# Attention scores of pass 2: from TensorE products to a VectorE turn, a DRAM reload and ScalarE's bias

## The chip, the core and the metric

One core of a Trainium2 chip. Its engines run side by side, each through its own list of instructions in order: TensorE (PE: matmuls, with weight loads, PEld, that overlap them), VectorE (DVE), ScalarE (ACT), GpSimd (POOL) and SyncE (SP), which here issues DMAs. They wait for each other by semaphores. The metric is the device time of one execution in microseconds (us), less is better. Before the change it is 2358.47 us, the median of three runs (2357.71 to 2360.64).

## What is computed

Two layers on `x` of 128 graphs x 64 nodes x 768 features, f32. Layer 0 is a graph convolution with relations; the change doesn't touch it. Layer 1 is graph attention with six heads of 128 features and a gate:

```python
h = jnp.einsum('bni,hio->bhno', feat_in, W)
th = jnp.tanh(h)
attn_src = jnp.einsum('bhno,hoz->bhnz', th, w_src)
attn_dst = jnp.einsum('bhno,hoz->bhnz', th, w_dst)
attn = attn_src + jnp.swapaxes(attn_dst, -1, -2)
attn = jnp.where(attn >= 0, attn, leaky_alpha * attn)
mask = (adj == 0)[:, None, :, :]
attn = jnp.where(mask, NEG_MASK, attn)
attn = jax.nn.softmax(attn, axis=-1)
feat_out = jnp.einsum('bhnm,bhmo->bhno', attn, h) + b
...
feat_out = jax.nn.elu(feat_out)
gate = jax.nn.sigmoid(feat_in @ H_w.T + H_b)
out = gate * feat_out + (1.0 - gate) * feat_in
```

A score is thus a sum: the source node's number plus the destination node's number, per head and graph, then leaky ReLU, mask and softmax over the 64 destinations.

## The kernel before

The 8192 nodes are 64 tiles of 128 rows (two graphs each), and two tiles are a pair: 32 pairs. Pass 1 (layer 0, up to about 1410 us) runs over all pairs and writes its results to DRAM. Pass 2 (layer 1) runs over the pairs again. Its work is cut into named steps, and one text, `ORDER` (line 104), gives the order in which they are issued in every iteration `i`: `name/k` means that the step is done for pair `i - k`. So an iteration works on several pairs at different stages. The list is complete (every step falls on a real pair) from iteration 4 to 29; `END` (line 122) is a second list for the last pairs. Steps of one engine run in the order of the list; between engines only data, buffers and semaphores decide. `FINISH` places the end of pass 1's last pair within the first iterations.

The steps, for a pair or, where a digit 0 or 1 follows the name, for one of its tiles:

- `ld` (load, load_h, lines 373 and 987): eight DMAs of 96 KB that bring a pair's transposed input h from DRAM in 128-byte pieces, and one for the adjacency `ai`. The step with pair p loads pair p + 1.
- `Ff..` (form, 1048): sums of input blocks on DVE. `P k.q` (half_product, 1055): 30 half products of 128x512 a pair on PE, 15 products by a fast-multiplication scheme for h and the gate together. They accumulate in PSUM banks a (two buffers), b, c and d, one bank running through several products: products 0, 3, 6, 9 and 12 use bank a. `R k` and `RA k` (read on DVE, 1077; read_act on ACT, 1073) read a bank between two of its products.
- `th` tanh on ACT (1095); `mul` one DVE product with both score vectors (1099); `sum` (1106): ACT's accumulating copies, `sum..0` and `sum..1` for the destination scores, `sum..2` and `sum..3` for the source scores.
- The scores: `k`, `chain` (1113, 1117, POOL): the scores split in three bf16 parts that add up to f32; `rows` (1139, PE): one bf16 matmul that turns them into rows; `rrow` (DVE) and `lrow` (ACT) lay the rows out as operands; `log` (1159, PE): one bf16 matmul that gives all scores of the tile, 128x384, in PSUM; `memset` (POOL) fills the mask's value, `cp` (1165, DVE) copies the unmasked scores over it; `pre` (1170, ACT) is the leaky ReLU.
- `tr` the negative maximum (DVE), `exp` (1178, ACT, six activations of 128x64 with sums), `rec` (DVE); `tv`, `ts`, `tl` (1201 to 1216): the weights are turned in 32x32 blocks on DVE, put to DRAM by four DMAs and loaded back turned, for the next step.
- `swap` (1126): two DMAs that swap the two graphs' halves of h; `att` (1242): 24 small matmuls with the pair's weights; `ev` (1254): twelve DVE evictions of 128x128, divided by the softmax sums; `e`, `g` on ACT; `f` (1273): three DVE steps; `lx` (996) loads the residual; `dma` (1284, POOL) adds the result to the output in DRAM.

Every DMA issue of SP takes its place in one queue: an issue whose data isn't ready holds all that stand behind it. Steps that the prediction follows by name: `P9.0`, `R6`, `R9`, `R12`, `att`, `ev`, `ld`, `Ff1`, `lx`, `ts`, `swap`, `tl`, `f1.2`, `f0.2`.

Of the kernel before, what the change touches and what calls it, by code (L numbers as in the profile page):

```python
# [101 lines left out]


ORDER = """
dma0/4 R1/1 RA1/1 P3.1/1 R2/1 memset1/2 R14/2 th1/2 R3/1 tv1/3 P11.0/1 rows0/2 P4.0/1 rrow0/2
lrow0/2 tl0/3 mul1/2 P6.0/1 Ff1 P4.1/1 R4/1 Ff6/1 log0/2 P6.1/1 P11.1/1 sum1.2/2 R6/1 sum1.3/2
sum1.0/2 Ff7 sum1.1/2 P7.0/1 k1/2 cp0/2 Ff4 lx1/3 P7.1/1 rec0/3 Ff2 P9.0/1 Ff8 Ff11/1 R7/1 P9.1/1
pre0/2 RA7/1 tr0/2 chain1/2 P8.0/1 Ff9 P8.1/1 R9/1 lx0/3 rows1/2 Ff10 memset0/1 ld R11/1 g1/3
exp0.0/2 ts1/3 rrow1/2 R8/1 P10.0/1 P10.1/1 exp0.1/2 Ff3 swap0/3 lrow1/2 th0/1 P12.0/1 tv0/2 R10/1
P12.1/1 mul0/1 tl1/3 g0/2 att/3 log1/2 R12/1 ev1.0/3 ev1.1/3 cp1/2 sum0.3/1 ev0.0/3 sum0.1/1 P13.0/1  # L110
e1/3 f1.0/3 P13.1/1 P14.0/1 sum0.0/1 P14.1/1 P2.0 P2.1 R13/1 ev0.1/3 P1.0 pre1/2 f1.1/3 sum0.2/1
tr1/2 f1.2/3 P0.0 P0.1 e0/3 dma1/3 P5.0 f0.0/3 swap1/2 P5.1 exp1.0/2 RA0 R0 P1.1 exp1.1/2 f0.1/3
ts0/2 RA5 k0/1 chain0/1 rec1/2 Ff5 RA14/1 P3.0 f0.2/3 R5 RA2
""".split()
# [3 lines left out]
END = """
g0/3 R1/2 R2/2 R14/3 Ff6/2 P3.1/2 Ff1/1 P11.0/2 R3/2 RA1/2 P4.0/2 rows0/3 P4.1/2 tv1/4 P6.0/2 th1/3
Ff11/2 rrow0/3 R4/2 lrow0/3 mul1/3 Ff4/1 sum1.2/3 P6.1/2 lx0/4 dma0/5 P7.0/2 rec0/4 sum1.1/3
sum1.0/3 P7.1/2 P8.0/2 log0/3 R6/2 Ff2/1 Ff8/1 Ff3/1 Ff7/1 Ff9/1 ts1/4 R7/2 swap0/4 P8.1/2 P9.0/2
k1/3 sum1.3/3 tl1/4 RA7/2 P9.1/2 Ff5/1 chain1/3 P11.1/2 R8/2 g1/3 P10.0/2 rows1/3 cp0/3 Ff10/1
pre0/3 P10.1/2 lrow1/3 R9/2 tr0/3 R11/2 memset1/3 th0/2 tl0/4 rrow1/3 att/4 log1/3 P12.0/2 P12.1/2
R10/2 P13.0/2 lx1/4 P13.1/2 mul0/2 exp0.0/3 ev1.0/4 ev1.1/4 sum0.3/2 ev0.0/4 ev0.1/4 e1/4 e0/4
sum0.2/2 P5.0/1 memset0/2 R12/2 g0/2 f1.0/4 cp1/3 P2.0/1 g1/4 P0.0/1 exp0.1/3 Ff6/1 swap1/3 f1.1/4
P14.0/2 P0.1/1 R13/2 pre1/3 f0.0/4 P14.1/2 sum0.0/2 f1.2/4 P1.0/1 f0.1/4 P2.1/1 R0/1 sum0.1/2 f0.2/4  # L130
RA0/1 RA2/1 R14/2 P1.1/1 RA1/1 P5.1/1 ld/1 P3.0/1 Ff11/1 R2/1 tr1/3 RA14/2 R1/1 RA5/1 R5/1 th1/2
tv0/3 mul1/2 exp1.0/3 P3.1/1 P8.0/1 Ff1 P8.1/1 exp1.1/3 k0/2 P4.0/1 dma0/4 chain0/2 tv1/3 ts0/3
sum1.1/2 rows0/2 rrow0/2 R3/1 sum1.2/2 lx1/3 P4.1/1 Ff2 Ff4 P11.0/1 lrow0/2 Ff5 P6.0/1 sum1.0/2
sum1.3/2 log0/2 P6.1/1 R4/1 k1/2 P7.0/1 cp0/2 Ff8 pre0/2 R6/1 P7.1/1 tr0/2 P9.0/1 exp0.0/2 ts1/3
R8/1 dma1/4 Ff3 P9.1/1 memset1/2 Ff9 rec0/3 R7/1 Ff10 Ff7 exp0.1/2 tv0/2 chain1/2 tl0/3 rows1/2
RA7/1 lrow1/2 P11.1/1 rrow1/2 lx0/3 P10.0/1 log1/2 swap0/3 tl1/3 R9/1 rec1/3 P10.1/1 R11/1 cp1/2
R10/1 th0/1 att/3 pre1/2 P13.0/1 mul0/1 sum0.3/1 ev1.1/3 ev0.0/3 memset0/1 sum0.1/1 sum0.2/1
sum0.0/1 lx0/2 ev1.0/3 ts0/2 ev0.1/3 P13.1/1 k0/1 P12.0/1 P12.1/1 tr1/2 chain0/1 R13/1 swap1/2 PH2
swap0/2 e1/3 R12/1 e0/3 PH0 P14.0/1 P14.1/1 f1.0/3 f0.0/3 f1.1/3 exp1.0/2 R14/1 exp1.1/2 tv1/2 PH5
f1.2/3 rows0/1 f0.1/3 RA14/1 lrow0/1 RAH0 dma1/3 f0.2/3 PH1 PG0 PH3 ts1/2 th1/1 RAH5 RAH1 RAH2  # L140
mul1/1 PH11 dma0/3 tl0/2 PH4 RH3 lx1/2 memset1/1 Ff6 sum1.0/1 RH4 Ff11 tl1/2 sum1.1/1 PH6 rrow0/1
PH7 RH6 sum1.3/1 RAH7 log0/1 PH9 RG0 sum1.2/1 cp0/1 RH9 pre0/1 rec0/2 RH11 PH8 RH8 PH10 th0 k1/1
chain1/1 rows1/1 att/2 lrow1/1 tr0/1 exp0.0/1 exp0.1/1 rec1/2 RH10 mul0 rrow1/1 PH13 log1/1 ev0.0/2
ev0.1/2 tv0/1 PH12 sum0.3 ev1.1/2 cp1/1 lx0/1 sum0.2 e0/2 sum0.0 pre1/1 RH12 ts0/1 f0.0/2 PG2 PH14
sum0.1 k0 RG2 PG3 RH13 tr1/1 PG1 PG8 swap0/1 exp1.0/1 ev1.0/2 f0.1/2 exp1.1/1 chain0 tl0/1 RAH14 RG3
rec0/1 rows0 PG6 f0.2/2 RG1 memset0 th1 swap1/1 tv1/1 e1/2 mul1 f1.0/2 rec1/1 lx0 f1.1/2 lrow0 PG4
g1/2 att0/1 rrow0 sum1.1 PG5 log0 dma0/2 f1.2/2 ev0.0/1 sum1.0 sum1.2 memset1 RG6 cp0 sum1.3 pre0
ts1/1 lx1/1 tl1/1 RG4 k1 chain1 rows1 ev0.1/1 e0/1 RG5 tr0 PG7 rrow1 lrow1 f0.0/1 g0/1 RG7 log1
f0.1/1 swap0 att1/1 PG11 cp1 exp0.0 f0.2/1 dma1/2 ev1.0/1 PG9 exp0.1 ev1.1/1 RG9 g1/1 swap1 pre1
turnp0 dma0/1 e1/1 tr1 PG10 PG12 RG10 f1.0/1 rec0 pT0 att0 f1.1/1 f1.2/1 exp1.0 RG12 PG14 RG8 exp1.1  # L150
ev0.1 turnp1 e0.1 rec1 PG13 ev0.0 f0.0.1 e0.0 RG14 RG11 RG13 pT1 f0.1.1 f0.0.0 g0 dma1/1 att1 f0.2.1
f0.1.0 lx1 ev1.1 g1 ev1.0 e1.1 f1.0.1 e1.0 f1.1.1 f1.0.0 f1.2.1 f1.1.0 f1.3.1 f1.2.0 f1.3.0 f0.2.0
out1.1 out0.1 out1.0 out0.0
""".split()


# [1 line left out]
def kernel(  # L158
# [90 lines left out]

# [153 lines left out]
    with ExitStack() as px:  # L403
        wa = px.enter_context(tc.tile_pool(name="wa", bufs=1))
        work = px.enter_context(tc.tile_pool(name="work0", bufs=2))
# [573 lines left out]
    with ExitStack() as px:  # L979
        wb = px.enter_context(tc.tile_pool(name="wb", bufs=1))  # L980
        work = px.enter_context(tc.tile_pool(name="work1", bufs=2))
# [225 lines left out]
        def put_blocks(t):  # L1207

            for f in range(NQ):
                nc.sync.dma_start(  # L1210
# [73 lines left out]
        def store(t):  # L1284
# [176 lines left out]
```

## Time and profile before

The profiled execution took 2358.5 us, its span from first to last instruction 2356.7 us. The granted TensorE clock was 0.994 over the span.

| view | PE | DVE | ACT | POOL |
|---|---|---|---|---|
| busy over the whole span, us | 2326.5 | 1979.0 | 1304.5 | 434.1 |
| share of the span | 99% | 84% | 55% | 18% |

| group in pass 2 | engine | mean of one, ns |
|---|---|---|
| half product's record, 128x512 f32 (two for each half product) | PE | 592 |
| `log`, 128x384 bf16, 64 of them | PE | 331 |
| `rows`, 128x192 bf16, 64 of them | PE | 249 |
| `mul`, 128x1536 | DVE | 1732 |
| `ev`, 128x128 | DVE | 331 |
| `rrow`, 64x384 | DVE | 531 |
| `cp`, 128x384 | DVE | 575 |
| `tv`, transpose of 128x384 | DVE | 567 |
| `exp`, 128x64 | ACT | 337 |
| `pre`, 128x384 | ACT | 509 |
| `lrow`, 18x128 | ACT | 257 |
| store to the output, issue | POOL | 887 |

A record's length is the time until its result is there; instructions of one engine overlap, so the distance from start to start is shorter (DVE by about 0.08 us). A timeline line gives the start, the length of a run of equal instructions, the engine, line, operation and tiles; `x4` means four of them. SPq and POOL with DMA_DIRECT2D are the issues of DMAs, not their transfers. The DMA queue that SP fills moved 269.11 MB in 696850 packets, its packets took 46.5% of the 16 DMA engines' span; POOL's queue took 6.0% with 24.78 MB.

### The profile page before, as it was taken

The page shows a single profiled execution, that of the slowest core. Times are in us where ns is not written, and L with a number is a line of the kernel's source. Part 1 is how long each engine was busy: PE and PEld are TensorE (multiplying, and loading weights), DVE is VectorE, ACT ScalarE, POOL GpSimd, SP SyncE. Part 2 cuts the span into 40 slices and gives each one's busy share as a digit, 9 for nine tenths or more (in the row PEclk, how much of TensorE's full clock was granted, in tenths as well). Part 3 has the DMA queues.
Part 4 walks back from the last instruction along what each step waited for, and adds up shares of the span by engine and source line. Part 5 has one row for each costly group of instructions (what it writes and reads, how often), then busy time and mean ns, then how long its engine had stood idle before and what let it go on. Part 6 is the DMA issues. An engine that isn't in the chain of part 4 may idle for free.

```text
span 2356.7 us, 35546 instructions
## 1 busy us (share of the span) xinstructions
PE 2326.5 (99%) x11591; PEld 1654.2 (70%) x11591; DVE 1979.0 (84%) x3673; ACT 1304.5 (55%) x3955; POOL 434.1 (18%) x983
## 2 busy tenths in 40 slices
PE   9999999999999999999999999999999999999996
PEld 7888888888888888888888885444444444444444
DVE  8878778777787787787787777899999999999997
ACT  3454454454554554554554533677766776777775
POOL 1111111111111111111111111122222222222222
PEclk9999999999999999999999999999999999999997
DMA  6334435335335335335334357577777776676776
GB/s 188 83 90 125 119 90 136 106 90 143 100 93 147 93 97 152 90 96 147 90 103 139 90 162 145 117 146 142 152 144 150 141 148 140 138 145 138 148 136 132
DMA packets 706907, 296.19 MB, mean 126 GB/s; under 512 B 524586, under 2 KB 657053, under 8 KB 706722
## 3 DMA queue, kind: packets, MB, share of 16 engines
q1 hardware_dynamic: 696850, 269.11, 46.5%
q0 software_dynamic: 9728, 24.78, 6.0%
q8 instruction: 91, 1.49, 0.3%
q14 instruction: 94, 0.77, 0.1%
q10 hardware_dynamic: 144, 0.04, 0.0%
HBM read 131.85 MB, written 136.45 MB: 114 GB/s over the span
## 4 chain that ended last, share of the span: by engine, by line
PE 94%; DVE 2%; DMA 2%; issue 1%; ACT 0%; SPq 0%; POOL 0%; POOLq 0%; DVEq 0%; ACTq 0%
PE pwa L754 21%; PE pwb L754 17%; PE pwcd L754 14%; PE pma L1059 13%; PE pmb L1059 11%; PE pmd L1059 5%; PE pmc L1059 4%; PE pb L682 3%; PE ps L1224 1%; PE pwcd L738 1%; PE pwcd L682 1%; DVE weights L353 1%; PE ps L1163 1%; DMA weights<-in_wrev_t_dram 1%; PE pmc L1224 0%
## 5 line engine op out<-in xcount | busy, mean ns | idle before, releaser
L754 PE MATMUL pwa<-weights,op 128*128 128x256 f32 x2304 | 539.4, 381 | 0.3 <-DVE x L746 0.3
L754 PEld LDWEIGHTS pwa<-weights,op 128*128 128x128 f32 x2304 | 422.3, 190 | 53.8 <-issue 1.1
L754 PE MATMUL pwb<-weights,op 128*128 128x256 f32 x1932 | 454.5, 381 | 0.0
L754 PEld LDWEIGHTS pwb<-weights,op 128*128 128x128 f32 x1932 | 359.4, 190 | 53.1 <-issue 0.2
L353 DVE TENSOR_TENSOR op<-op 128x768 f32<-128x768 f32 x310 | 291.5, 949 | 95.6 <-ACT op L692 91.7
L754 PE MATMUL pwcd<-weights,op 128*128 128x256 f32 x1560 | 357.8, 379 | 0.0
L754 PEld LDWEIGHTS pwcd<-weights,op 128*128 128x128 f32 x1560 | 296.1, 190 | 40.1
L1059 PE MATMUL pma<-weights,op_f 128*128 128x512 f32 x620 | 291.2, 592 | 0.0
L1111 ACT ACTIVATE pr<-pr 128x128 f32<-128x128 f32 x768 | 225.6, 295 | 92.3 <-DVE pr L1101 90.5
L692 ACT COPY op<-pb 128x512 f32<-128x512 f32 (+1 forms) x132 | 70.8, 618 | 320.5 <-PE pb L682 320.5
L1059 PEld LDWEIGHTS pma<-weights,op_f 128*128 128x128 f32 x620 | 117.7, 190 | 147.4 <-issue 139.0
L330 POOL TENSOR_SCALAR rn<-su 128x1 f32<-128x1 f32 x124 | 28.1, 227 | 901.9 <-ACT hf L325 531.0
L1059 PE MATMUL pmb<-weights,op_f 128*128 128x512 f32 x372 | 180.9, 594 | 0.0
L540 ACT ACTIVATE hp<-x,rn 128x768 f32<-128x768 f32 x60 | 107.8, 1797 | 109.7 <-POOL rn L332 109.7
L1111 ACT ACTIVATION_READ_ACCUMULATOR pr<-pr 128x1 f32 x768 | 143.6, 187 | 0.0
L324 ACT ACTIVATE hf<-x 128x768 f32<-128x768 f32 x64 | 53.6, 837 | 150.1 <-DVE x L790 150.1
L1184 ACT ACTIVATE pb<-al,mx 128x64 f32<-128x64 f32 x384 | 128.1, 336 | 12.3 <-DVE mx L1176 12.2
L1059 PEld LDWEIGHTS pmb<-weights,op_f 128*128 128x128 f32 x372 | 68.4, 190 | 84.0 <-issue 75.8
L1285 POOL DMA_DIRECT2D out_dram<-f x62 | 55.0, 887 | 390.0 <-DVE f L1282 382.6
L746 DVE TENSOR_TENSOR x<-pwa,x 128x256 f32<-128x256 f32 x96 | 40.4, 421 | 99.8 <-PE pwa L738 72.0
L1059 PE MATMUL pmb<-weights,h 128*128 128x512 f32 x248 | 122.5, 596 | 0.0
L1059 PE MATMUL pmc<-weights,op_f 128*128 128x512 f32 x248 | 121.8, 592 | 0.0
(232 smaller groups left out, 4219.3 us busy)
## 6 DMA issues: line engine op xcount, KB each, us to landing
x<-in_x_dram SPq DMA_DIRECT2D x64, 384.0 KB
h<-ht SPq DMA_DIRECT2D x64, 384.0 KB
out_dram<-x SPq DMA_DIRECT2D x64, 384.0 KB
hh<-hh SPq DMA_DIRECT2D x64, 384.0 KB
h<-h SPq DMA_DIRECT2D x256, 96.0 KB
x<-hh SPq DMA_DIRECT2D x64, 384.0 KB
out_dram<-f POOLq DMA_DIRECT2D x62, 384.0 KB, 6.5
h<-hpt SPq DMA_DIRECT2D x60, 384.0 KB
```

The costliest lines, as they stand in the source:

```text
L324: nc.scalar.activation(by, src, AF.Copy, scale=-1.0 / D, accum_out=sums[:, 0:1])
L330: nc.gpsimd.tensor_scalar(to[:, 0:1], sums[:, 1:2], 1.0 / D, EPS, op0=OP.mult, op1=OP.add)
L353: return (nc.vector.tensor_add if s1 == "+" else nc.vector.tensor_sub)(to, x, y)
L540: nc.scalar.activation(hp.rearrange("p (b f i) -> p b f i", b=KB, f=NQ), X[t].rearrange("p (b i f) -> p b f i", b=KB, f=NQ), AF.Relu, scal ...
L682: nc.tensor.matmul(to[:, g, :, i, :], H0[2 * p + k][o, kb * P : (kb + 1) * P], rts[p % 2][o, k, :n].rearrange("p s n -> p (s n)"), start=T ...
L692: nc.scalar.copy(a[:, :n].rearrange("p s h (g n) -> p g (s h) n", g=GT), ps[:, :, c * n * KQ * N : (c + 1) * n * KQ * N].rearrange("p g (x ...
L746: nc.vector.tensor_add(v, bank[b][:, :CQ], v)
L754: nc.tensor.matmul(bank[b][:, :CQ], OPS[p, an][:, s, q, :], bw[bn][:, (s * KQ + q) * CQ : (s * KQ + q + 1) * CQ], start=(first and q == s ...
L1059: nc.tensor.matmul(bank[p, b], operand(p, an)[:, q, :], bw2[bn][:, 2 * q * CQ : 2 * (q + 1) * CQ], start=(first and q == 0), stop=(q == KQ ...
L1111: nc.scalar.activation(PR[t][:, j, h, :], PR[t][:, j, h, :], AF.Copy, accum_out=to)
L1184: nc.scalar.activation(PB[t][:, h, :], AL[t][:, h, :], AF.Exp, bias=MX[t][:, h : h + 1], accum_out=DN[t][:, h : h + 1])
L1285: nc.gpsimd.dma_start(of[t * P : (t + 1) * P, :], FF[t], accum_op=OP.add)
```

## The change

For pairs 0 to 29 (`BY_PE = 2` leaves the last two) the scores no longer go over PE. The destination scores are summed into a 128x32 tile; `sv` transposes it on DVE in 32x32 blocks; `ss` puts it to DRAM with four DMAs of six partitions x 128 bytes; `sl` loads it back with two DMAs, each of which spreads one 1536-byte row over 64 partitions (96 KB); `lk` adds the source score as the bias of ACT's leaky ReLU, one activation for each head; `cl` copies the unmasked results over the mask's value. `k`, `chain`, `rows`, `rrow`, `lrow`, `log`, `cp` and `pre` remain for the last two pairs. All three order texts are new; in `ORDER`, `ld` now has k = 1 (before: 0).

```diff
+    BY_PE = 2
...
+    SDD = [dram.tile([GT, H * N], F32, name=f"sd_{t}") for t in range(NT)]
...
+        sdt = []
+        for i in range(2):
+            sd = wb.tile([P, Q], F32, name=f"sdt{i}")
+            nc.gpsimd.memset(sd, 0.0)
+            sdt.append(sd)
...
-            SD[t] = small.tile([P, 2, H], F32, name="sd")
+            SD[t] = sdt[t % 2] if t // 2 < NP - BY_PE else small.tile([P, 2, H], F32, name="sd")
...
-                to = SD[t][:, 1, h : h + 1] if j else SG[t][:, 2, h : h + 1]
+                to = (SG[t][:, 2, h : h + 1] if not j else SD[t][:, h : h + 1] if t // 2 < NP - BY_PE
+                      else SD[t][:, 1, h : h + 1])
...
+        def turn_scores(t):
+            ST[t] = work.tile([P, Q], F32, name="st2")
+            nc.vector.transpose(ST[t], SD[t])
+
+        def put_scores(t):
+            for f in range(NQ):
+                nc.sync.dma_start(
+                    SDD[t].rearrange("g (h f n) -> g f h n", h=H, f=N // Q)[f // 2, f % 2],
+                    ST[t][f * Q : f * Q + H])
+
+        def get_scores(t):
+            DR[t] = work.tile([P, H, N], F32, name="dr")
+            for g in range(GT):
+                nc.sync.dma_start(DR[t][g * N : (g + 1) * N].rearrange("p h n -> p (h n)"),
+                                  SDD[t][g : g + 1, :].to_broadcast([N, H * N]))
+
+        def leaky_sum(t):
+            PB[t] = work.tile([P, H, N], F32, name="pb")
+            for h in range(H):
+                nc.scalar.activation(PB[t][:, h, :], DR[t][:, h, :], AF.Prelu, alpha=LEAKY,
+                                     bias=SG[t][:, 2, h : h + 1])
+
+        def choose_leaky(t):
+            AL[t] = AM[t]
+            nc.vector.copy_predicated(AM[t], AI[t // 2][:, t % 2, None, :].to_broadcast([P, H, N]),
+                                      PB[t])
...
-            nc.gpsimd.memset(AM[t], NEG_MASK / LEAKY)
+            nc.gpsimd.memset(AM[t], NEG_MASK if t // 2 < NP - BY_PE else NEG_MASK / LEAKY)
...
-            al = AL[t] = work.tile([P, H, N], F32, name="al", bufs=1)
+            al = AL[t] = work.tile([P, H, N], F32, name="al", tag="dr")
...
+            "rec": one_over, "sv": turn_scores, "ss": put_scores, "sl": get_scores, "lk": leaky_sum, "cl": choose_leaky,
```

The list of an iteration afterwards (the one before is in the listing above):

```
lk1/3 f1.1/4 g0/2 R13/2 e0/4 f1.2/4 memset1/3 P1.0/1 cl1/3 Ff5/1 R0/1 RA0/1 ld/1 tr1/3 f0.0/4 P5.0/1
P5.1/1 exp1.0/3 P3.0/1 lx0/3 P1.1/1 P3.1/1 f0.1/4 RA5/1 R5/1 f0.2/4 exp1.1/3 Ff6/1 sum0.2/2 R14/2
RA1/1 sl0/2 RA2/1 tv1/3 P11.0/1 R1/1 ts1/3 lx1/3 RA14/2 P11.1/1 swap0/3 P4.0/1 swap1/3 P4.1/1 th1/2
lk0/2 R2/1 Ff11/1 R3/1 tl0/3 mul1/2 R4/1 Ff1 rec0/3 sum1.0/2 P8.0/1 P6.0/1 Ff8 sum1.1/2 P6.1/1 cl0/2
R6/1 Ff4 sum1.3/2 P7.0/1 dma1/4 Ff2 P7.1/1 P9.0/1 RA7/1 tl1/3 Ff7 sv1/2 P9.1/1 tr0/2 ss1/2 exp0.0/2
P8.1/1 Ff3 Ff9 exp0.1/2 R7/1 R9/1 R11/1 R8/1 P10.0/1 tv0/2 rec1/3 dma0/4 sum1.2/2 th0/1 P10.1/1
P12.0/1 memset0/1 R10/1 ts0/2 att/3 P12.1/1 P13.0/1 mul0/1 sum0.0/1 ev1.1/3 sum0.1/1 R12/1 ev1.0/3
P2.0 ev0.0/3 ev0.1/3 g1/2 P14.0/1 e1/3 P14.1/1 sv0/1 f1.0/3 sl1/2 sum0.3/1 P13.1/1 Ff10 P2.1 P0.0
ss0/1 P0.1
```

SP's own order within it, read as a cycle that begins at the list's end: `ss0` (4 DMAs), `ld` (9), `lx0` (1), `sl0` (2), `ts1` (4), `lx1` (1), `swap0` and `swap1` (4), `tl0` (1), `tl1` (1), `ss1` (4), `ts0` (4), `sl1` (2). Before: `ts1` (4), `swap0` (2), `tl1` (1), `swap1` (2), `ts0` (4), `tl0` (1), `lx1`, `lx0` (2), `ld` (9).

More of the change, by code (lines that the diff above doesn't have):

```diff
@@ L104 @@
 ORDER = """
[L105 to L110, printed above, removed]
@@ L111 @@
-e1/3 f1.0/3 P13.1/1 P14.0/1 sum0.0/1 P14.1/1 P2.0 P2.1 R13/1 ev0.1/3 P1.0 pre1/2 f1.1/3 sum0.2/1
-tr1/2 f1.2/3 P0.0 P0.1 e0/3 dma1/3 P5.0 f0.0/3 swap1/2 P5.1 exp1.0/2 RA0 R0 P1.1 exp1.1/2 f0.1/3
-ts0/2 RA5 k0/1 chain0/1 rec1/2 Ff5 RA14/1 P3.0 f0.2/3 R5 RA2
+lk1/3 f1.1/4 g0/2 R13/2 e0/4 f1.2/4 memset1/3 P1.0/1 cl1/3 Ff5/1 R0/1 RA0/1 ld/1 tr1/3 f0.0/4 P5.0/1
+P5.1/1 exp1.0/3 P3.0/1 lx0/3 P1.1/1 P3.1/1 f0.1/4 RA5/1 R5/1 f0.2/4 exp1.1/3 Ff6/1 sum0.2/2 R14/2
+RA1/1 sl0/2 RA2/1 tv1/3 P11.0/1 R1/1 ts1/3 lx1/3 RA14/2 P11.1/1 swap0/3 P4.0/1 swap1/3 P4.1/1 th1/2
@@ L114 @@
 """.split()
-FINISH = (158, 189, 215, 216, 242, 268)
+FINISH = (168, 179, 185, 210, 259, 281)
 END = """
[L123 to L151, printed above, removed]
@@ L152 @@
-f0.1.0 lx1 ev1.1 g1 ev1.0 e1.1 f1.0.1 e1.0 f1.1.1 f1.0.0 f1.2.1 f1.1.0 f1.3.1 f1.2.0 f1.3.0 f0.2.0
-out1.1 out0.1 out1.0 out0.0
+e0/5 P5.0/2 f1.1/5 R13/3 tl0/4 sum0.2/3 P1.0/2 f0.0/5 lk1/4 memset1/4 f1.2/5 f0.1/5 f0.2/5 RA0/2
+P1.1/2 R0/2 R1/2 cl1/4 R2/2 dma0/5 P5.1/2 RA1/2 ld/2 tr1/4 RA2/2 R14/3 exp1.0/4 rec0/4 Ff5/2 R5/2
+exp1.1/4 sl0/3 P3.0/2 RA14/3 P3.1/2 P4.0/2 R3/2 Ff6/2 P4.1/2 R4/2 tv1/4 th1/3 Ff11/2 P6.0/2 RA5/2
+Ff1/1 P6.1/2 lk0/3 P7.0/2 lx1/4 dma1/5 mul1/3 sum1.3/3 P11.0/2 R6/2 P7.1/2 ts1/4 swap1/4 sum1.1/3
@@ new lines @@
+P11.1/2 cl0/3 RA7/2 rec1/4 Ff5/1 Ff8/1 tr0/3 P9.0/2 Ff9/1 P9.1/2 R7/2 sum1.0/3 Ff7/1 Ff10/1 P8.0/2
+sv1/3 P8.1/2 Ff2/1 swap0/4 exp0.0/3 sum1.2/3 P10.0/2 tl1/4 P10.1/2 R9/2 Ff3/1 R11/2 R8/2 th0/2 Ff4/1
+ss1/3 R10/2 mul0/2 P12.0/2 att/4 ev1.0/4 P13.0/2 sum0.0/2 P13.1/2 P12.1/2 exp0.1/3 P5.0/1 lx0/4
+ev1.1/4 ld/1 P2.0/1 memset1/3 e1/4 ev0.0/4 ev0.1/4 sum0.1/2 f1.0/4 e0/4 sl1/3 sum0.2/2 R13/2 sv0/2
+P0.0/1 f0.0/4 P2.1/1 f1.1/4 R12/2 f1.2/4 P1.0/1 P0.1/1 g0/2 P5.1/1 lk1/3 f0.1/4 R0/1 P14.0/2 RA5/1
+cl1/3 P14.1/2 f0.2/4 g1/3 RA0/1 RA14/2 memset0/2 tr1/3 tv0/3 swap1/3 P1.1/1 P3.0/1 RA1/1 P3.1/1 R1/1
@@ new lines @@
+Ff6/1 P4.0/1 Ff1 exp1.0/3 exp1.1/3 R2/1 ss0/2 R5/1 RA2/1 P4.1/1 sl0/2 R14/2 sum0.3/2 P11.0/1 tv1/3
+R3/1 th1/2 Ff11/1 R4/1 lk0/2 mul1/2 ts0/3 g0/3 ts1/3 dma0/4 sum1.0/2 Ff7 dma1/4 memset1/2 P6.0/1 Ff2
+cl0/2 P8.0/1 P7.0/1 P6.1/1 Ff8 P7.1/1 P8.1/1 R6/1 sum1.1/2 sv1/2 RA7/1 lx1/3 Ff9 swap0/3 P9.0/1
+tl0/3 tr0/2 tl1/3 Ff10 R8/1 P9.1/1 R7/1 Ff4 sum1.2/2 exp0.0/2 R9/1 sum1.3/2 exp0.1/2 P11.1/1 ss1/2
+R11/1 rec1/3 rec0/3 att/3 th0/1 P10.0/1 Ff3 P12.0/1 tv0/2 P10.1/1 P12.1/1 mul0/1 ev1.1/3 PH0 ev1.0/3
@@ new lines @@
+sum0.0/1 ev0.0/3 sl1/2 sum0.3/1 R10/1 ts0/2 e1/3 f1.0/3 sum0.2/1 R12/1 sum0.1/1 lk1/2 ev0.1/3 PH5
+f1.1/3 P14.0/1 lx0/3 cl1/2 g0/1 f1.2/3 P13.0/1 P13.1/1 tr1/2 P14.1/1 e0/3 k0/1 swap0/2 RAH0 tl0/2
+f0.0/3 chain0/1 R14/1 RAH5 exp1.0/2 exp1.1/2 R13/1 RA14/1 f0.1/3 th1/1 tv1/2 PH3 f0.2/3 PH2 PH1
+rows0/1 memset1/1 PH11 memset0/1 mul1/1 RAH1 lrow0/1 RAH2 PH4 sum1.0/1 RH3 PG0 dma0/3 swap1/2 Ff5
+PH6 RH4 Ff6 Ff11 rrow0/1 dma1/3 sum1.1/1 sum1.3/1 PH7 RG0 k1/1 rec0/2 ts1/2 log0/1 sum1.2/1 PH8
+lx0/2 RH6 RAH7 cp0/1 PH9 pre0/1 RH8 chain1/1 PH10 tr0/1 RH9 RH10 rows1/1 rrow1/1 rec1/2 g1/1
@@ new lines @@
+exp0.0/1 RH11 PH12 lrow1/1 RH12 log1/1 exp0.1/1 cp1/1 tv0/1 tl1/2 rec0/1 att/2 pre1/1 ts0/1 tr1/1
+ev0.1/2 ev0.0/2 ev1.0/2 PH14 e0/2 lx1/2 ev1.1/2 exp1.0/1 memset0 PG2 f0.0/2 RAH14 swap0/1 PG3 f0.1/2
+exp1.1/1 lx0/1 tl0/1 f0.2/2 e1/2 tv1/1 f1.0/2 PH13 th0 mul0 ts1/1 RH13 g1/2 dma0/2 sum0.0 sum0.1
+sum0.2 sum0.3 th1 RG2 PG5 f1.1/2 RG3 rec1/1 swap1/1 f1.2/2 att0/1 PG1 RG1 k0 PG6 RG5 RG6 ev0.0/1
+ev0.1/1 dma1/2 tl1/1 chain0 lx0 mul1 PG4 e0/1 PG8 f0.0/1 RG4 memset1 rows0 lrow0 PG11 f0.1/1 rrow0
+lx1/1 PG9 att1/1 PG7 sum1.2 sum1.1 f0.2/1 log0 sum1.0 k1 cp0 sum1.3 dma0/1 ev1.1/1 chain1 ev1.0/1
@@ L154 @@
+pre0 e1/1 tr0 exp0.0 rows1 RG7 RG8 f1.0/1 rrow1 f1.1/1 swap0 lx1 lrow1 exp0.1 RG9 f1.2/1 PG10 log1
+turnp0 PG12 cp1 RG11 pT0 pre1 g0 att0 RG10 rec0 tr1 dma1/1 RG12 swap1 exp1.0 ev0.0 e0.0 exp1.1 PG14
+ev0.1 e0.1 f0.0.0 RG14 PG13 f0.1.0 turnp1 pT1 RG13 f0.0.1 rec1 att1 f0.1.1 f0.2.0 g1 f0.2.1 ev1.1
+ev1.0 e1.1 f1.0.1 out0.1 e1.0 f1.1.1 f1.0.0 out0.0 f1.2.1 f1.1.0 f1.3.1 f1.2.0 f1.3.0 out1.1 out1.0
 """.split()
@@ L1091, in hz @@
             return (hzs[t % NHZ][:, 0, :].rearrange("p (h o) -> p h o", h=H), hzs[t % NHZ][:, 1, :])
-        TH, PR, SD, SG, PS, AM, AL, PB, DN, MX, PT, PO, FF, EE, HX, TP = ({} for _ in range(16))
+        TH, PR, SD, SG, PS, AM, AL, PB, DN, MX, PT, PO, FF, EE, HX, TP, ST, DR = ({} for _ in range(18))
         def tanh(t):
@@ L1180, in exps @@
             if i == 0:
-                PB[t] = work.tile([P, H, N], F32, name="pb")
+                if t // 2 >= NP - BY_PE:
+                    PB[t] = work.tile([P, H, N], F32, name="pb")
                 DN[t] = small.tile([P, H], F32, name="dn")
@@ L1290 @@
             "lx": load_x, "log": logits, "cp": choose, "pre": leaky, "tr": largest,
-            "rec": one_over, "tv": turn_blocks, "ts": put_blocks, "tl": get_blocks, "turnp": turn_p, "pT": copy_p,
+            "rec": one_over, "sv": turn_scores, "ss": put_scores, "sl": get_scores, "lk": leaky_sum, "cl": choose_leaky,
+            "tv": turn_blocks, "ts": put_blocks, "tl": get_blocks, "turnp": turn_p, "pT": copy_p,
             "att": attend, "g": gate, "e": exp_f,
```

## The prediction

> **What bounds the kernel now.** I read four views, from coarse to fine: busy time of each engine over two of pass 2's periods; TensorE's timeline around the two score products; the queue of SyncE (SP), which issues nearly all DMAs; and how full the DMA engines are behind one burst of loads.
>
> ```profile
> core 0: us, PE busy (x) PEld busy (x) DVE busy (x) ACT busy (x) POOL busy (x), PEclk, DMA share, GB/s
> 1891.70:1919.50 27.80, 27.80 (x113) 12.80 (x112) 26.90 (x57) 19.65 (x88) 7.03 (x16) 1.00 0.71 145
> 1919.50:1947.40 27.90, 27.90 (x113) 12.84 (x112) 27.00 (x57) 19.65 (x88) 7.05 (x16) 1.00 0.71 144
> ```
>
> A period (one pair of tiles, from one `att` to the next) takes 27.88 us. TensorE (PE) has no gap in it, at full clock. VectorE (DVE) is busy 27.0 of it, ScalarE (ACT) 19.65. So a period is TensorE's own work, and what leaves TensorE shortens it until something else arrives last.
>
> ```profile
> 1908.88 0.33 PE L1163 MATMUL ps<-rrow,lrow 82*128 82x384 bf16 x1
> 1909.04 1.02 PE L1059 MATMUL pma<-weights,h 128*128 128x512 f32 x2
> ...
> 1914.19 1.88 PE L1059 MATMUL pmd<-weights,op_f 128*128 128x512 f32 x4
> ...
> 1915.91 0.25 PE L1144 MATMUL ps<-idr,sdb 128*82 128x192 bf16 x1
> ...
> 1915.99 1.91 PE L1059 MATMUL pmb<-weights,op_f 128*128 128x512 f32 x4
> ```
>
> Read starts, not lengths: the matmul after `logits` starts 0.16 us after it, the one after `rows` 0.08. Four f32 records take 1.88, the last one 0.59 (its group's mean), so they start 0.43 apart and a half product (two records) is 0.857. Check: 60 x 0.429 = 25.72, plus 2 x 0.24 = 0.48 for the scores, leaves 1.68 for `att`, together 27.88.
>
> ```profile
> 195.01 6.46 SPq L306 DMA_DIRECT2D dl<-ident  x9
> 1463.07 4.97 SPq L378 DMA_DIRECT2D h<-h  x8
> 1468.77 1.18 SPq L1130 DMA_DIRECT2D hx<-weights  x2
> 1899.84 0.95 SPq L999 DMA_DIRECT2D x<-hh  x2
> 1900.64 0.88 POOL L1285 DMA_DIRECT2D out_dram<-f  x1 [13.42 <-DVE f L1282]
> 1900.85 10.99 SPq L378 DMA_DIRECT2D h<-h  x8
> 1904.86 0.88 POOL L1285 DMA_DIRECT2D out_dram<-f  x1 [0.30 <-DVE hz L1088]
> 1912.50 1.96 SPq L1210 DMA_DIRECT2D pt<-tp  x4
> ```
>
> The same eight h loads hold SP for 4.97 us when little else moves and 10.99 when two x loads stand ahead and two stores run beside. A DMA of six partitions (`dl`) costs SP 0.718, one of 32 (`pt`) 0.49.
>
> ```profile
> DMA  9996000999999999999999981000066660005998
> h<-h SPq DMA_DIRECT2D x11, 96.0 KB
> hx<-weights SPq DMA_DIRECT2D x2, 192.0 KB
> ai<-in_adj_dram SPq DMA_DIRECT2D x1, 64.0 KB
> ```
>
> These are half-microsecond slices from 1460. The eight h loads issued at 1463.07, then ai, then hx keep the DMA engines at nine tenths until 1472; the completion event of the second hx is at 1473.20, 10.13 us after the first h issue. Completions come in the order of issue there: what is issued behind h lands behind h.
>
> **The change part by part.** The sum is made against the profiled execution's 2358.5 us (span 2356.7 and 1.8 around it); the median of the runs is 2358.47.
>
> *Leaves PE:* 0.24 for each of 60 tiles (pairs 30 and 31 keep the products): 14.4 us, 0.48 in a period, so 27.40. The written list is full in 26 iterations: 12.5 us there, 1.9 before and after.
>
> *Off the path by load:* DVE loses two `rrow` (530 ns, following ones start 0.08 earlier than they end: 0.45 each) and gains two 128x32 transposes. No row has these; between the reciprocal's 0.18 and the 128x384 transpose's 0.57 I take 0.2. DVE falls to 26.3 of 27.4. ACT loses `pre` (0.41) and `lrow` (0.16) and gains six 128x64 activations a tile; the exps of that size take 336 ns with starts 0.24 apart (without the accumulator's read), so +0.87 a tile, 21.4. POOL loses `k` and `chain` (0.46 + 3 x 0.27 + 2 x 0.5 = 2.3 a tile). The DMA engines gain 384 KB in a period. No engine becomes the bound by its load.
>
> *SP gains 12 DMAs in a period (25 become 37), and here is the cost.* After the change SP's list runs: `ss0` (four puts), `ld` (eight h loads, ai), `lx0`, `sl0`, `ts1`, `lx1`, four swaps, `tl0`, `tl1`, `ss1`, `ts0`, `sl1`. SP issues in order. `ss0` waits for `sv0` on DVE, which stands behind the evictions `ev` of `att`; queued behind it is all of `ld` and then `sl0`, for which ACT's `lk0` waits, for which DVE's `cl0` waits; straight behind `cl0` stands `R6`, and PE's P9.0 writes on in the bank that `R6` reads. That is a closed loop of one period. Its links:
> - P9.0 to `att`: six half products, 5.14.
> - `att` 1.68, P12.1 0.86, handover to DVE 0.26 (R9: matmuls end their slot at 1914.20, DVE starts at 1914.46), R12 0.60, nine evictions of 0.258 (2.32): 5.72.
> - `sv0` with its handover 0.25.
> - `ss0`: six partitions each, so by the `dl` row 4 x 0.718 = 2.87; by the `pt` row 4 x 0.49 = 1.96. I take the first, whose partitions are the same number.
> - S, from the first h issue to the landing of `sl0`.
> - `lk0` 1.53, `cl0` 0.57 (574 ns), R6 0.69: 2.79.
>
> Without S: 16.8. For S, eight h, ai, one x (384 KB) and two `dr` loads (192 KB) must move. From below, the 1463 row: 10.13 for eight h, ai and 384 KB; 192 KB more at the some 200 GB/s that the window's last slices show is 0.95: 11.1. From above, the 1899.84 row: x, x, h, ai with both stores beside complete at 1914.56, 14.7; one x less (384 KB, 1.9 at the same rate) and two `dr` more: 13.8. So two stores cost 2.7. Where are the stores afterwards? DVE reaches `f1.2` 9.4 after `att` (evictions, `sv0`, f1.0, a form, f1.1, R13, f1.2) and `f0.2` 13.9 after it; `ld` starts at 8.84. Stores at +0.5 and +5.0 stand as they do in the upper row. I count one in full, as the second may drain behind `sl0`: S = 12.45. The loop is 29.2, longer than PE's 27.40, so the period is 29.2: +1.32 x 26 = 34, less 1.9 outside: **2391 us**. Break-even is S = 11.1 (27.88), its lower bound.
>
> *Moved:* `ld` loads the pair that the same iteration uses (`Ff1`, DVE); before, the loads had a whole period of cover, hidden by PE's products. The same loop through `Ff1` instead of `sl0`: 5.14 + 5.72 + 0.25 + 2.87 + 8.3 (last h complete after 8.28 in the 1463 row) + Ff1, rec0, Ff8, cl0, R6 (2.1) = 24.4; with a store 25.8. It costs nothing as long as that stays under 27.4. The source score now comes straight as a bias and `cl` reads SBUF where `cp` read PSUM; I count that at nothing, within DVE's 1.0 of slack.
>
> [...]
>
> **Rivals.**
> - *PE stays the bound (faster).* The loop stays under 27.40: S at its lower bound 11.1 and puts at the `pt` row give 27.0. For it: SP stood idle for 9.1 of 27.88 us (18.8 busy), and x no longer stands ahead of h. Against: both stores fall into S. Time: 2358.5 - 14.4 = 2344. Decides where the loop is below 27.40.
> - *Nothing measurable.* The loop ends within 0.17 of 27.88: 2354 to 2363. A measurement of this kernel can't tell less than 0.2%, 4.7 us, from no change.
> - *The queue's tail decides (slower still).* Behind `sl0` stand `ts1`, `lx1`, the swaps, `tl0` and `tl1`, and `att` waits for `tl1`: 8.84 + loads + 0.6 + 0.5 + 1.15 + 2.1 + 0.5 + 2.3 + 0.4 + 2.7 (pT's completion) = 19.1 + loads. With 10.99, as at 1900.85, that is 30.1: 2358.5 + 57.7 - 1.9 = 2414. With 4.97 it is 24.1 and hides. Against: the 10.99 had two x loads ahead.
>
> **How the numbers follow.** My forecast 0.52, the queue's tail 0.14, PE-bound 0.27, nothing measurable 0.07. Faster 0.27, same 0.07, slower 0.66. The forecast's own range is 2365 (loop 28.2) to 2429 (S = 13.8, loop 30.6). With 27 in 100 at 2344, the range reaches down to it: 2342 to 2429.
>
> **What would show it.** Right: periods of `att` near 29 us; PE idle in each, before a pma product, released by a DVE read of pma (R6); ACT idle before the Prelu on `dr`, released by the DMA; puts of 0.7 us each on SP; h loads shorter than 10 us. Wrong in size: the wait there but other lengths of the h loads or landings. Wrong altogether: PE without a gap and periods of 27.40, or gaps released by anything that doesn't lead back to SP's queue.

## The result, and the profile after

The changed kernel is slower: 2396.11 us, the median of four runs (2391.67 to 2404.11), against 2358.46 for the kernel before on the same chip; the ratio is 1.0162, 95% interval 1.0134 to 1.0190. The profiled execution took 2396.1 us, its span is 2394.3.

The first view is the busy time of the engines in one period (from one `att` to the next) and in two short stretches that are read at the end of this document.

```profile
core 0: us, PE busy (x) PEld busy (x) DVE busy (x) ACT busy (x) POOL busy (x), PEclk, DMA share, GB/s
1827.80:1857.55 29.75, 27.69 (x113) 12.46 (x112) 26.16 (x57) 20.77 (x97) 2.57 (x4) 1.00 0.76 149
1911.00:1913.70 2.70, 2.41 (x4) 1.16 (x5) 2.70 (x9) 2.70 (x18) 0.00 (x0) 0.69 1.07 212
1913.70:1918.00 4.30, 4.30 (x9) 1.63 (x7) 3.15 (x7) 3.01 (x15) 0.42 (x1) 0.80 0.15 31
```

TensorE, which had no gap before (27.80 of 27.80 us busy), is now idle for 2.06 of 29.75 us. DVE and ACT have the loads that were expected (26.3 and 21.4 forecast, 26.16 and 20.77 here); neither is the bound. The next view is the timeline around that idle time, of PE, ACT and DVE those lines that make the chain.

```profile
1848.23 1.88 PE L1066 MATMUL pmb<-weights,op_f 128*128 128x512 f32 x4
1849.39 1.54 ACT L1145 ACTIVATE pb<-dr,sg 128x64 f32<-128x64 f32 x6 [5.60 <-DMA dr<-sd]
1850.96 0.59 DVE L1150 COPY_PREDICATED a<-ai,pb 128x384 f32<-128x384 int32 x1 [3.42 <-ACT pb L1145]
1851.45 0.67 DVE L1095 TENSOR_TENSOR hz<-hz,pma 128x512 f32<-128x512 f32 x1
1852.17 0.30 PEld L1066 LDWEIGHTS pma<-weights,op_f 128*128 128x128 f32 x2 [2.89 <-DVE hz L1095]
1852.17 1.98 PE L1066 MATMUL pma<-weights,op_f 128*128 128x512 f32 x4 [2.06 <-DVE hz L1095]
```

Read it from the end upwards. PE starts P9.0 at 1852.17 after 2.06 us of nothing, released by a DVE read of bank a (`R6`). That read stands behind `cl0` (L1150), for which DVE waited 3.42 us on ACT's `lk0` (L1145), for which ACT waited 5.60 us on the reload `sl0`. The reload's place is in SP's queue, shown next for the same period.

```profile
1833.69 1.29 SPq L1130 DMA_DIRECT2D sd<-st  x4
1835.02 4.59 SPq L380 DMA_DIRECT2D h<-h  x8
1839.66 0.84 SPq L995 DMA_DIRECT2D ai<-in_adj_dram  x1
1840.54 1.78 SPq L1001 DMA_DIRECT2D x<-hh  x1
1842.42 1.31 SPq L1138 DMA_DIRECT2D dr<-sd  x2
1843.83 2.91 SPq L1251 DMA_DIRECT2D pt<-tp  x4
1846.78 0.51 SPq L1001 DMA_DIRECT2D x<-hh  x1
1847.39 3.14 SPq L1170 DMA_DIRECT2D hx<-weights  x4
1850.58 1.24 SPq L1257 DMA_DIRECT2D pT<-pt  x2
```

`sl0` (L1138) is issued 7.40 us after the first h load and has landed when ACT starts, 14.37 after it. Between the first h issue and that landing the two stores go out, as POOL's queue shows for the same period:

```profile
1837.47 0.86 POOL L1326 DMA_DIRECT2D out_dram<-f  x1 [10.87 <-DVE f L1323]
1842.12 0.86 POOL L1326 DMA_DIRECT2D out_dram<-f  x1 [3.79 <-DVE f L1323]
```

Last, the sums of the waits between 1530 and 2250 us (engine, tile and line; what it waited for; total, times, longest). They show that the period above is the rule: the last two rows are `R6` with either of its targets, and make 38.9 of the 39.4 us in which TensorE is idle in this stretch.

```profile
ACT pb L1145 <- DMA dr<-sd: 123.8, 25, 6.0
...
DVE a L1150 <- ACT pb L1145: 72.1, 24, 3.8
...
PEld pma L1066 <- DVE weights L1095: 40.8, 28, 3.1
PE pma L1066 <- DVE weights L1095: 24.6, 16, 2.3
...
PE pma L1066 <- DVE hz L1095: 14.3, 8, 2.5
```

Cut at the same events, the medians of 21 periods (the fifth to the twenty-fifth of the list) stand beside the forecast like this; the landing of `sl0` is taken from ACT's start, 0.02 us later:

| link of the loop | forecast, us | measured, us |
|---|---|---|
| `att` to the first put of `ss0` (`att`, evictions, `sv0`) | 5.97 | 5.91 |
| four puts of `ss0` | 2.87 | 1.33 |
| S: first h issue to `sl0` there | 12.45 | 13.84 (12.65 to 14.74) |
| `lk0` to the next `att` (`lk0`, `cl0`, `R6`, P9.0 to `att`) | 7.93 | 8.19 |
| sum | 29.2 | 29.27 |

The median period is 29.39. The 26 periods of the full list took 769.5 us where they took 724.9, +44.6; ahead of the first `att` 2.0 us were gained, behind the last 5.0 (125.49 against 130.44). Together that is +37.6, the difference of the spans.

### The profile page after: what moved, and what is told of

It is laid out like the page before. It is cut to its first block, busy times and chain, and to the rows that moved or that the text cites. A ratio compares the mean times of both kernels' runs of the same rounds, so it can differ in the third digit from the quotient of the medians.

```text
span 2394.3 us, 35519 instructions
## 1 busy us (share of the span) xinstructions
PE 2325.0 (97%) x11471; PEld 1645.2 (69%) x11471; DVE 1956.4 (82%) x3673; ACT 1339.8 (56%) x4195; POOL 305.6 (13%) x625
## 5 line engine op out<-in xcount | busy, mean ns | idle before, releaser
L1066 PE MATMUL pma<-weights,op_f 128*128 128x512 f32 x620 | 309.7, 606 | 43.4 <-DVE weights L1095 29.1
L1145 ACT ACTIVATE pb<-dr,sg 128x64 f32<-128x64 f32 x360 | 92.1, 334 | 141.3 <-DMA dr<-sd 141.3
L1225 ACT ACTIVATE pb<-a,mx 128x64 f32<-128x64 f32 x360 | 120.4, 336 | 6.5 <-DVE mx L1216 3.0
L635 DVE TENSOR_REDUCE sum<-eq 128x26 f32<-128x1664 bf16 x64 | 120.0, 1875 | 0.1
```

What stands on the lines that cost most here:

```text
L635: nc.vector.tensor_reduce(SUM[p][:, k], EQ[p, k], AX.X, OP.add)
L1066: nc.tensor.matmul(bank[p, b], operand(p, an)[:, q, :], bw2[bn][:, 2 * q * CQ : 2 * (q + 1) * CQ], start=(first and q == 0), stop=(q == KQ ...
L1145: nc.scalar.activation(PB[t][:, h, :], DR[t][:, h, :], AF.Prelu, alpha=LEAKY, bias=SG[t][:, 2, h : h + 1])
```

## The experiments

The question was which of four things makes the loop: the place of `sl0` behind the h loads, the lost cover of the moved `ld`, the queue's tail behind `sl0`, or simply the added traffic. S and the time from `att` to the landing of the last weights (`tl1`) are medians of the same 21 periods; the mean period is that over 22.

| run | time, us (range) | ratio to before, 95% | mean period | what PE waits for in the profile |
|---|---|---|---|---|
| changed kernel | 2396.11 (2391.67–2404.11) | 1.0134–1.0190 | 29.57 | `R6`, that is `sl0` |
| `ld` early | 2411.16 (2408.72–2415.77) | 1.0210–1.0242 | 29.89 | `R6` |
| `sl0` first | 2392.12 (2387.86–2398.68) | 1.0125–1.0166 | 29.24 | weights at `att`, and reads behind `Ff1` |
| both | 2395.77 (2389.81–2404.69) | 1.0132–1.0192 | 29.21 | weights at `att` |
| reload by ACT's queue | 2407.74 (2404.61–2409.98) | 1.0193–1.0227 | 29.78 | weights at `att`; `R6` little |
| spread | 2360.16 (2357.32–2364.59) | 1.0000–1.0020 | 28.08 | weights at `att`, 8.2 us in all |
| puts that wait for nothing | 2339.82 (2337.78–2341.04) | 0.9906–0.9935 | 27.46 | nothing of note |
| `lk` without `sl` | 2367.10 (2359.69–2370.33) | 1.0023–1.0045 | 28.66 | weights at `att` |
| no stores | 2334.80 (2334.64–2335.23) | 0.9886–0.9915 | 27.42 | nothing of note |
| late stores | 2414.75 (2404.16–2417.30) | 1.0229–1.0257 | 29.89 | weights at `att` |
| moved and late | 2339.14 (2339.04–2340.01) | 0.9907–0.9934 | 27.43 | nothing of note |
| moved alone | 2424.86 (2418.44–2425.47) | 1.0261–1.0289 | 30.87 | `R6` |

### The cover of `ld`, and the place of `sl0`

The first run loads a pair one iteration earlier than it is used, as before the change, but at `ld`'s new place:

```diff
             elif n == "ld":
-                load(p + 1)
+                if p + 1 == 4:
+                    load(4)
+                load(p + 2 if p + 1 >= 4 else p + 1)
```

> Edit: from iteration 4 on, ld loads the next pair instead of the one that the same iteration uses; its place in SP's queue, between ss0 and sl0, stays. Theory (the loop through SP's queue to sl0): S, from the first h issue to the landing of sl0, stays near 13.8 us, the period near 29.5, the time 2396 (2388 to 2404). Rival, lost cover (Ff1's wait for h sets the period): the wait is gone, periods of 27.4, 2340. Rival, traffic or order (the extra DMA bytes, or the new order of DVE's and ACT's work, set it): 2396 too.

The median period is 29.38, S is 13.91 and ACT waits for `dr` as before (125.6 us in the 720, against 123.8): the lost cover isn't the cause. (The time is even longer; the clock records, read at the end, have 31 us at half clock between 1520 and 2250 against 10.) The second run puts `sl0` straight behind `ss0`, ahead of `ld` (and drops the one `sl0` of the last list that is thereby done):

```diff
-RA1/1 sl0/2 RA2/1
+RA1/1 RA2/1
...
-ss0/1 P0.1
+ss0/1 sl0/1 P0.1
```

> Edit: sl0 is issued straight behind ss0, ahead of ld. Theory: sl0 lands some 5 us after ss0 starts; its loop is 5.15 + 5.91 + 1.33 + 1.2 (landing of the puts) + 1.1 + 2.5 + 2.8 = 20 us and no longer counts. ld starts some 2.3 later, so the loop through Ff1 is 5.15 + 5.91 + 1.33 + 2.3 + 9.6 to 10.5 + 2.1 = 26.4 to 27.3: TensorE bounds again, periods of 27.4 to 27.8, 2340 to 2350. Rival, lost cover: h lands later than now, so slower than 2396. Rival, traffic or order: 2396.

> Edits: sl0 straight behind ss0, and ld one pair ahead. Theory: both loops through SP are under 27.4, TensorE bounds with periods of 27.40, 26 x 2.16 = 56 us less than the changed kernel: 2340 (2336 to 2346). Rival, traffic or order: 2390 or more.

Both missed their 2340. ACT's wait for the reload is gone from the waits of the second run, and two others stand in its place:

```profile
DVE op_f L355 <- DMA h<-h: 39.0, 22, 2.7
...
PEld ps L1265 <- DMA pT<-pt: 33.4, 30, 2.9
```

DVE's `Ff1` now waits for the h loads, which `sl0` pushed back and which have no cover any more; and `att` waits for its weights. With the cover restored as well (the run with both), only the second remains:

```profile
PEld ps L1265 <- DMA pT<-pt: 47.3, 31, 7.3
...
PE ps L1265 <- DMA pT<-pt: 29.7, 44, 6.5
```

So the theory of a single path was too simple: the tail of SP's queue is a second path of almost the same length. In the changed kernel the last weights land 28.58 after `att`, in a period of 29.39: 0.8 us to spare. (`att` begins with the other tile's weights; in the runs that it bounds, the last weights land 0.5 to 0.6 us behind its start.)

### Another queue

```diff
-                nc.sync.dma_start(DR[t][g * N
+                (nc.sync if t % 2 else nc.scalar).dma_start(DR[t][g * N
```

> Edit: the two reloads of sl0 are issued by ScalarE, on its own DMA queue, at the same place of the list; sl1 stays with SP. Theory (what counts is standing behind h in SP's queue): the reload no longer waits for the h loads' issue nor lands behind them, lk0's wait goes, periods of 27.4 to 28.3, 2340 to 2365. Rival, traffic (the DMA engines are full in that stretch, on whichever queue): S stays above 12, 2385 or more.

The wait for the reload is shorter (73.6 us instead of 123.8 in the same 720; S falls to 12.38), but the weights now land 30.12 after `att`, and `att` waits for them: 32.3 of TensorE's 36.0 us of idle time. Why the tail became longer isn't shown. Neither expectation has its mechanism: the time and an S above 12 are what the traffic theory named, but the next run excludes that theory.

### Traffic or waiting

In the first of these runs the four puts read a constant tile, so that SP needn't wait for `sv0`; every DMA and every byte stays.

```diff
-                    ST[t][f * Q : f * Q + H])
+                    wsd[f * Q : f * Q + H, 0, :Q])
```

> Edit to the changed kernel: the puts take their data from a constant tile instead of the transposed scores (the destination scores are left out; every DMA and every byte stays). SP no longer waits for sv0. Theory: SP runs ahead as it did before the change, TensorE bounds, periods of 27.4 to 27.8, 2340 to 2350. Rival, traffic: 2385 or more.

```profile
1530.00:2250.00 720.00, 720.00 (x2824) 331.51 (x2823) 695.37 (x1473) 553.90 (x2516) 66.93 (x104) 1.00 0.86 162
```

PE is busy for all of the 720 us while the DMA engines carry 162 GB/s, more than in the changed kernel's period above (149). The DMA engines carry the whole traffic in 27.46 us a period here; that SP stands still until `sv0` is done (95.2 us of waits for both tiles' turned scores in the changed kernel's 720) is what makes it late. The second run leaves everything in place but lets `lk` read a constant tile instead of the reload:

```diff
-nc.scalar.activation(PB[t][:, h, :], DR[t][:, h, :], AF.Prelu, alpha=LEAKY,
+nc.scalar.activation(PB[t][:, h, :], wsd[:, 0, : H * N].rearrange("p (h n) -> p h n", h=H)[:, h, :], AF.Prelu, alpha=LEAKY,
```

> Edit to the changed kernel: lk reads a constant tile instead of the reloaded scores (the destination scores are left out of the sum; all DMAs stay). ACT and DVE wait for nothing of SP there; SP still waits for sv0. Theory with both paths: the path over the queue's tail to tl1 and att stays, periods near 29, 2385 to 2396. Theory with the path over sl0 alone: 2340. Rival, traffic on the DMA engines as such: 2385 or more.

It came out between the two expectations. With the `sl0` path cut, the period is 28.66 and `att` waits for its weights: this is the tail's own length in this kernel, 0.9 shorter than the changed kernel's 29.57 and 1.2 longer than PE's work.

### The stores

```diff
-            nc.gpsimd.dma_start(of[t * P : (t + 1) * P, :], FF[t], accum_op=OP.add)
+            if t >= NT - 4:
+                nc.gpsimd.dma_start(of[t * P : (t + 1) * P, :], FF[t], accum_op=OP.add)
```

> Edit to the changed kernel: the final store of all but the last four tiles is left out (their output is incomplete). Theory: without two stores beside it S falls by some 2.7 us to 11.1, the loop to 26.3, the tail's path by as much; TensorE bounds, 2338 to 2350. If the stores don't lengthen S: near 2396.

S falls from 13.84 to 9.43 us (9.15 to 10.36), the last weights land 25.44 after `att`, and the period is PE's:

```profile
1530.00:2250.00 720.00, 720.00 (x2826) 331.16 (x2825) 696.18 (x1474) 553.64 (x2516) 21.76 (x52) 1.00 0.66 133
```

The two stores thus cost S 4.4 us. The run whose puts wait for nothing fits in between: there the stores stand 5.7 and 10.3 us after the first h issue, the second shortly before S ends, and S is 11.7.

### Towards a better order

The run "spread" has both earlier edits, and issues the four swaps and the first weight reload of the next `att` ahead of `ss0`, in the time in which SP waits for `sv0` (the list for the last pairs drops the steps that are thereby done):

```diff
-f1.0/3 sl1/2 sum0.3/1
+f1.0/3 sl1/2 swap0/2 swap1/2 tl0/2 sum0.3/1
...
-P11.1/1 swap0/3 P4.0/1 swap1/3 P4.1/1
+P11.1/1 P4.0/1 P4.1/1
...
-R3/1 tl0/3 mul1/2
+R3/1 mul1/2
```

> Edits: those of both, and the four swaps and tl0 are issued in the stretch in which SP waits for sv0, ahead of ss0, so that only ss0, sl0, ld, lx0, ts1, lx1 and tl1 stand between sv0 and att. Theory (two paths through SP's queue begin at the wait for sv0, one to lk0, one to tl1 and att; both are now shorter by more than 2 us): TensorE bounds, periods of 27.4 to 27.9, 2338 to 2352, faster than both kernels. Rival, traffic: the same bytes in a period, so 2385 or more.

It gives back 36 of the 38 us but doesn't beat the kernel before: TensorE still waits at `att`, 8.2 us in all in the 720, 7.2 of it for weights. That this is because the tail still has both stores is not shown by this run; the last three move the stores. A copy of one element on POOL holds each store until the reload of the same iteration is there; "late stores" is the changed kernel with this alone:

```diff
+            if 0 <= t // 2 < NP - BY_PE - 4:
+                lt = small.tile([1, 1], F32, name="lt")
+                nc.gpsimd.tensor_copy(lt, DR[t // 2 * 2 + 4][:1, 0, :1])
             nc.gpsimd.dma_start(of[t * P : (t + 1) * P, :], FF[t], accum_op=OP.add)
```

> Nothing is left out. For pairs 0 to 25 each store is held back on POOL by a one-element copy of the destination scores that the same iteration reloads (sl0), so that the two stores start only after that reload has landed, instead of 2.4 and 7.1 us after the first h issue. Theory (S is stretched by the two stores, the tail behind sl0 has some 3.5 us of room when no store is in flight): S falls towards what it is without stores, PE is again the bound in most periods and the time is 2336 to 2352. The other theory (the queue's tail is as long as the sl0 path, and stores cost the same wherever they fall): the stores now meet the two loads of the weights, att waits for those in many periods, and the time is 2360 or more.

S did fall, to 9.39, but the second theory was right: the stores now run into the tail, whose last weights land 29.86 after `att` (28.58 before this edit), and `att` waits for them. These are SP's issues and two rows of the waits:

```profile
1889.14 4.29 SPq L380 DMA_DIRECT2D h<-h  x8
...
1894.63 1.09 SPq L1138 DMA_DIRECT2D dr<-sd  x2
1897.14 1.88 SPq L1251 DMA_DIRECT2D pt<-tp  x4
1899.07 0.47 SPq L1001 DMA_DIRECT2D x<-hh  x1
1899.64 3.72 SPq L1170 DMA_DIRECT2D hx<-hz  x4
1903.40 4.15 SPq L1257 DMA_DIRECT2D pT<-pt  x2
```

```profile
PEld ps L1265 <- DMA pT<-pt: 58.4, 30, 4.3
...
ACT pb L1145 <- DMA dr<-sd: 16.1, 24, 1.7
```

The two weight reloads take SP 4.15 us to issue here (median of the 21 periods 2.92), where the changed kernel's took 1.24 (1.26). "Moved and late" adds to this the three edits of the list shown for "spread" (with `ld` and `sl0` left where the change has them), and "moved alone" has these three without the late stores:

> As the run with the late stores, and besides the four swaps and the first reload of the weights are issued one period earlier in real time, before ss0, while SP waits there for the transposed scores. Behind sl0 there remain ts1, lx1 and tl1, so the tail is some 3 us shorter. If the tail is what late stores cost, this is 2336 to 2345, below both kernels, with att waiting for no landing; if the moved transfers lie in front of the h loads and lengthen S, ACT waits for sl0 as before and the time is 2360 or more.

> The changed kernel with the four swaps and the first reload of the weights issued ahead of ss0, as in the run before, but with the stores where the changed kernel has them. Nothing is left out. If the two stores inside S are what makes the sl0 path too long, S stays near 13.8, ACT waits for sl0 in nearly every period, periods stay at 29 or more and the time is 2380 to 2400: then only both edits together help, the late stores for the sl0 path and the move for the tail. If the shorter queue is what helped and the stores may stand anywhere, the time is 2337 to 2350.

Together they give 2339.14 us, 0.8% below the kernel before and 2.4% below the changed one; each alone is slower than the changed kernel. (With the late stores alone the median period, 29.41, is that of the changed kernel; the mean is 0.3 longer, with four stretches at half clock instead of three.) Here is the combination's window, and its SP queue:

```profile
1530.00:2250.00 720.00, 720.00 (x2826) 331.28 (x2825) 696.40 (x1474) 552.80 (x2516) 84.67 (x154) 1.00 0.82 162
```

```profile
1889.79 1.68 SPq L1130 DMA_DIRECT2D sd<-st  x4
1891.52 4.31 SPq L380 DMA_DIRECT2D h<-h  x8
1895.87 0.53 SPq L995 DMA_DIRECT2D ai<-in_adj_dram  x1
1896.44 0.47 SPq L1001 DMA_DIRECT2D x<-hh  x1
1897.01 1.11 SPq L1138 DMA_DIRECT2D dr<-sd  x2
1899.11 1.87 SPq L1251 DMA_DIRECT2D pt<-tp  x4
1901.03 0.48 SPq L1001 DMA_DIRECT2D x<-hh  x1
1903.31 0.38 SPq L1257 DMA_DIRECT2D pT<-pt  x1
```

Behind `sl0` there are six DMAs instead of eleven; S is 9.53, the last weights land 25.74 after `att`, and both are in time for a period of 27.42. Moved alone, S stays at 13.79, the puts start 0.3 and end 0.65 us later than in the changed kernel (behind the swaps), and `R6` is later still.

## Why the prediction was right, and where it was not

- **The direction and the place: right, and shown.** PE waits before a product on bank a for `R6`, behind `cl0`, `lk0` and the landing of `sl0`, as the loop said. Cutting the loop at SP's wait for `sv0` brings the time to 2339.8, where the forecast put the case in which PE is the bound: 2344.
- **The puts: the wrong row.** The forecast took 0.718 each because `dl` also has six partitions. They take 0.33 (1.33 for four), less than the 0.49 of the 32-partition row. The number of partitions didn't make them dear. Why each `dl` issue took 0.718 stays open. That step was 1.54 too long.
- **S: too short, and for two wrong reasons that partly cancel.** The lower bound of 11.1 was no bound: without stores S is 9.43. And the stores cost 4.4 together, where the row gave 2.7 and the forecast counted half of it. It also had them at +0.5 and +5.0 after the first h issue; they stand at +2.4 and +7.1, mainly since the puts were shorter and so `ld` came 1.6 earlier, further ahead of them. Counting both as the upper bound did (13.8) would have hit the measured 13.84, but by luck, as that 13.8 has the same two errors.
- **So the path was right, and the sum of 29.2 by luck**: two errors (−1.54 and +1.39) cancel; the time of 2391 is 5 us from the median. The rest: 26 periods cost 44.6 instead of 34, since their mean is 29.60 and not 29.2, and outside them 6.9 us were gained instead of 1.9. What gained the 5.0 behind the last `att` wasn't tried; the list for the last pairs is a new one too. The top of the range, 2429, leaves out the 1.9 that the other sums take off; with it it is 2427.
- **`ld` without cover costs nothing here: right** (the run with early loads has the same median period), but only as long as `sl0` stays behind it: with `sl0` first, `Ff1` waits (39.0 us in the 720).
- **The rival of the queue's tail was better than its 0.14.** It was priced as a period of 30.1; alone it is 28.66 and lies 0.9 behind the path that decided. No edit of the `sl0` path alone could gain more than that 0.9, which is why `sl0` first, the pair of both edits and ACT's queue missed. Its size came close for a wrong reason: the 30.1 needed h loads that hold SP for 10.99 us. They hold it for 4.5, with which its own sum gives 23.6, a tail that hides. What it had too short is the rest: in the changed kernel 11.6 us pass from the last h issue to the issue of `tl1` and 5.2 more to its landing, where the sum had 7.6 and 2.7.
- **The rival of PE as the bound** named S and the puts as its condition. With the stores out of S and the shorter tail it is real: 27.43 a period, 2339.

## What to carry to other kernels

When work is moved from an engine to a queue that issues in order, follow both ways through that queue: what the moved step itself waits for, and what stands behind it with its own due time; if the two are of nearly equal length, mending one gains nothing, and only edits to both show anything (here 2414.75 and 2424.86 us alone, 2339.14 together). Price a wait on a landing by what else is in flight then: here two stores from another engine's queue, which appear nowhere in SP's list, made 4.4 of 13.8 us. Before giving up such a change, look for an engine's or a queue's idle wait into which transfers can be issued that are already ready, and hold back the ones that nobody waits for.

## What the runs showed of the hardware that was not expected

Some periods are longer by 1.7 us than their gap explains. In the changed kernel they are the three that contain a stretch at half of TensorE's clock (a granted share of 0.50 in the trace's clock records): they take 31.87, 31.47 and 31.65 us, and without the gap 29.22 us are left of each, where the periods beside them leave 27.52. This is one in PE's timeline; the two stretches from 1911.00 in the first view above have a mean granted clock of 0.69 and 0.80:

```profile
1907.14 1.88 PE L1066 MATMUL pmb<-weights,op_f 128*128 128x512 f32 x4
1911.29 3.10 PE L1066 MATMUL pma<-weights,op_f 128*128 128x512 f32 x4 [2.27 <-DVE weights L1095]
```

Four records (two half products) take 3.10 us there instead of 1.88. By the trace's clock records, each stretch lasts 3.413 us and they begin at 1673.1, 1703.8 and 1912.0, that is 9 and 70 times 3.413 apart: on a raster. In "moved alone" there are eight, some of double length, 37.5 us between 1530 and 2250; its median period is 30.21, its mean 30.87:

```profile
1858.66 1.88 PE L1066 MATMUL pmb<-weights,op_f 128*128 128x512 f32 x4
1864.85 3.78 PE L1066 MATMUL pma<-weights,op_f 128*128 128x512 f32 x4 [4.32 <-DVE hz L1095]
```

Gaps of 2.25, 2.43 and 2.65 us (from the last matmul's slot to the next start) were followed by a halved stretch in the changed kernel, while one of 2.38 was not, and in "moved alone" gaps up to 3.26 were not. The length of a gap alone thus doesn't say which ones a halved stretch follows; what tells them apart in these traces is how it falls on the raster. In the changed kernel the part of a gap that lay within one step of 3.413 us was 2.08, 2.25 and 2.43 us ahead of the three halved stretches and at most 2.01 elsewhere (1.82 for the gap of 2.38); in "moved alone" it was 2.04 to 3.38 ahead of the eight and at most 2.04 elsewhere (1.87 for that of 3.26). No run moved a gap on the raster by itself. In the changed kernel three waits of 2.25 to 2.65 us thus go with a further 1.7 us of their periods each.
